# Layer 2's end columns on GpSimd, Scharr smoothing from two-row sums, x2 stored in a step of its own, and new step lists in a four-layer convolution kernel

## The chip, the cores and the metric

The kernel runs on one core of a Trainium2 chip. The metric is the time of one execution on the device in microseconds, median of several runs. Names used below: PE is TensorE, DVE is VectorE, ACT is ScalarE, POOL is GpSimd, SP is the engine that here only issues DMAs. POOL issues DMAs too.

## What is computed

The input x is 16 images of 64 channels with 128 x 128 points, float32. Four layers follow, each of the form x = x + f(gn(x)), with gn a group norm over pairs of channels.

```python
# layer 0: gram = xf xf^T / N ; f = conv_w (gram xf)
# layer 1: f = |Kx * v| + |Ky * v|,  Kx = [[3,0,-3],[10,0,-10],[3,0,-3]], Ky = Kx^T up to sign
# layer 2: temporal shift (a quarter of the channels one column left, a quarter one right), 3x3 conv, + b
# layer 3: y = 3x3 conv with w_bin, 1x1 conv, batch norm over all 16 images, leaky relu, clip(0, 255)
```

Layer 3's batch norm needs the sums over all images, so the last part of it can start only when every image has passed the 3x3 convolution.

## The kernel before, in words

**Tiles.** An image is cut into 8 tiles of R = 8 rows per half image; 128 partitions are 64 channels times two halves. Each image passes four stages, one tile or one pair of tiles per step of the main loop: Gram (products for layer 0), Front (layers 0 and 1, one tile a step; `x`, `po`, `xh`, `u`, `e` are its tiles), Layer2 and Layer3 (two tiles a step; `v`, `dA`, `dB`, `q`, `one`, `two`, `c`). Several images are under way at once. From step FIRST + LAG on, the work repeats every eight steps, that is once per image: four steps with pairs of Layer 2, called (False, 0) to (False, 3) in the code and F0 to F3 here, then (True, 3), (True, 0), (True, 1), (True, 2) with pairs of Layer 3, T3, T0, T1, T2 here. Front works on tile 0 of an image in T1, tile 1 in T2, tiles 2 to 5 in F0 to F3, tile 6 in T3, tile 7 in T0. After the last step comes the tail: batch norm coefficients, the end of layer 3 read back from HBM, and for six images (`AGAIN`) layer 3's convolution a second time (`v_again`, `two_again`).

**Order of the work.** The dictionary ORDER (line 27) gives each kind of step a list of parts; `for name in ORDER[kind_of(step)]` (line 1282) calls the parts in that order, and every engine and every DMA queue runs its instructions in the order in which they were called (class InOrder, line 124; all operations go through its line 134, so the profile shows L134 for nearly all of them). "a" and "b" are the first and second tile of a pair: "load a" and "load b" fetch tiles for the pair after next, "near a", "near b" and "far a" norm them, "d a" and "d b" form the differences, "a one", "a own" and "section" are the matmuls, "a sum" adds the partial results, "a sq" squares for the statistics, "a out" stores. "stencil", "smooth", "slope", "abs", "x +", "+ y" are the six parts of Scharr. "0" to "3" are four phases in which Gram and the chains of small products advance.

**Scharr** (line 736). "stencil" makes u = 3 v[1:R+2] + v[0:R+1] on R + 1 rows, 128 x 1170 elements, and e = v[2:R+2] - v[0:R], 128 x 1040. "smooth" makes u = 3 u + u[next row], which is 3, 10, 3 over three rows, and a first step of the column smoothing of e. "slope" takes differences, "abs" is on ACT, "x +" and "+ y" add x and the two absolute values; the result, x2, lies in the tile u, of which there are two buffers.

**x2's store** (part "x2" in Front.at, line 682, and Front.store, line 766). In the step after the one that made it, x2 is stored with two DMAs issued by SP, and in the same part ACT squares it. A buffer of u may be written again only when its store and its square are done.

**Gram's loads** (line 571). In the second step of an image's Gram the first three loads (`xr`, 512 KB each) are issued by SP together in phase 0; each further one follows the use of an earlier one.

**Layer2.norm** (line 957). ACT norms a loaded tile of (R + 1) rows. The temporal shift needs two corrections: the two end columns, times a channel mask, go into a tile `edges`, 9 rows for either side (two ACT instructions), and in the tile itself the first and last column are multiplied by masks (two more). **Layer2.combine** (line 1022) adds `edges` to the end columns of `two` in PSUM, in two DVE instructions because the lower 64 partitions take rows 1 to 8 and the upper ones rows 0 to 7, and then forms x3. `different` (line 929) takes the difference of neighbouring rows of the normed tile on DVE and, for the second of a pair, copies part of it with two DMAs issued by POOL (`q`). `one` (line 984) is the first matmul on the normed tile.

**The tail's first norm** (line 1334). In phase 2 of the last step the first tile of the second pass is normed by ACT (`again_in`, line 1225).

Of the kernel before, what the change touches and what calls it, by code (L numbers as in the profile page):

```python
# [10 lines left out]
F32 = mybir.dt.float32  # L11
AF = mybir.ActivationFunctionType
# [12 lines left out]
PARTS = SCHARR + ("x", "mix", "mix b", "rows a", "rows b", "x2")  # L25
# [3 lines left out]
        "a one", "0", "x", "rows b", "load a", "stencil", "mix", "a c", "b sum", "a own", "b sq", "wi",  # L29
        "near b", "smooth", "slope", "1", "x2", "section", "close", "d b", "a sum", "b one", "abs", "rows a",  # L30
        "x +", "2", "b out", "a out", "b own", "a sq", "b c", "mix b", "mean", "scale", "far a", "d a",
        "load b", "+ y", "3",
    ],
    (False, 1): [
        "x", "rows b", "a one", "load a", "b sum", "0", "stencil", "b sq", "wi", "mix", "a c", "near b", "x2",
        "smooth", "a own", "close", "slope", "section", "b out", "abs", "rows a", "1", "d b", "a sum", "mean",
        "2", "x +", "b one", "a out", "mix b", "b c", "scale", "a sq", "b own", "far a", "d a", "load b", "+ y",
        "3",
    ],
    (False, 2): [  # L40
        "x", "rows b", "a one", "load a", "stencil", "b sum", "smooth", "0", "a c", "mix", "a own", "b sq",
        "wi", "near b", "x2", "close", "b out", "section", "slope", "1", "b one", "d b", "mean", "abs",
        "rows a", "a sum", "far a", "x +", "2", "mix b", "b c", "scale", "a sq", "a out", "d a", "load b",
        "+ y", "b own", "3",
    ],
    (False, 3): [
        "x", "rows b", "a one", "load a", "stencil", "b sum", "0", "mix", "a c", "a own", "b sq", "wi",
        "smooth", "near b", "slope", "section", "b out", "close", "x2", "d b", "mean", "a sum", "abs", "rows a",
        "a out", "1", "x +", "2", "load b", "b one", "d a", "+ y", "b own", "mix b", "b c", "a sq", "scale",
        "3",  # L50
    ],
    (True, 3): [
        "rows b", "stencil", "x2", "a one", "load a", "0", "b sum", "b sq", "mix", "a own", "smooth", "a c",
        "close", "mean", "scale", "slope", "b out", "x", "section", "1", "abs", "near a", "near b", "rows a",
        "b one", "b c", "a sum", "x +", "2", "b own", "load b", "wi", "a sq", "a out", "mix b", "+ y", "d a",
        "d b", "3",
    ],
    (True, 0): [
        "rows b", "x2", "a one", "a own", "b sum", "0", "stencil", "b sq", "load a", "smooth", "close", "a c",
        "near a", "mean", "slope", "x", "1", "mix", "section", "abs", "near b", "rows a", "wi", "b out", "2",  # L60
        "b one", "b c", "a sum", "scale", "x +", "b own", "far a", "d a", "d b", "a sq", "a out", "+ y",
        "load b", "mix b", "3",
    ],
    (True, 1): [
        "a one", "x2", "rows b", "load a", "b sum", "a own", "0", "stencil", "near b", "b sq", "close",
        "smooth", "d b", "a c", "slope", "1", "b out", "x", "mix", "section", "mean", "scale", "abs", "rows a",
        "2", "a sum", "x +", "wi", "b one", "b c", "b own", "d a", "a sq", "a out", "+ y", "load b", "mix b",
        "3",
    ],
    (True, 2): [  # L70
        "rows b", "a one", "b sum", "0", "stencil", "b sq", "load a", "x2", "1", "smooth", "a own", "close",
        "mean", "slope", "b out", "x", "a c", "near a", "mix", "abs", "section", "near b", "b one", "b c",
        "rows a", "a sum", "wi", "2", "x +", "a sq", "load b", "scale", "a out", "b own", "far a", "d a", "d b",
        "+ y", "mix b", "3",
    ],
    "fill": [
        "x", "a one", "b sum", "rows b", "load a", "stencil", "0", "a own", "b sq", "x2", "mix", "smooth",
        "slope", "b out", "close", "near b", "section", "d b", "a c", "mean", "1", "rows a", "wi", "abs",
        "a sum", "x +", "mix b", "b one", "2", "+ y", "b c", "a out", "load b", "b own", "d a", "a sq", "scale",
        "3",  # L80
# [90 lines left out]
def tile_kernel(ctx: ExitStack, tc: tile.TileContext, x, cw_h, w2_t, b2, wbin_t, w1_t, b1, gamma, beta, consts, out):  # L171
# [10 lines left out]
    def k(name):  # L182
        return kc[:, AT[name][0]:AT[name][1]]
# [75 lines left out]
    def chunk_tile(name):  # L259
        return ring.tile([P, (R + 2) * W], F32, tag="v", name=name, bufs=4)  # L260
# [296 lines left out]
    class Gram:  # L557
# [5 lines left out]
        def at(self, i, q):  # L563
            b = self.b
            n = 4 * (i - NS) + q

            self.part({1: 44, 5: 42, 9: 42}.get(n, 0))
            if n == 10:
                chains.append(gram_chain(b, self.pg))

            if i == 1 and q == 0:
                for m in range(3):
                    self.load(m)
            m = {11: 0, 13: 1, 15: 2, 17: 3, 19: 4, 21: 5, 23: 6, 25: 7}.get(4 * i + q)
            if m is not None:
                rows_to_columns(b, m, self.xr.pop(m))
                if m + 3 < NS:
                    self.load(m + 3)
# [45 lines left out]
    class Front:  # L624
        first, last = -3, NS

        def __init__(self, b):
            self.b, self.xs, self.po, self.x2 = b, {}, {}, {}

            self.four = b >= EARLY  # L630
            self.st = stp.tile([P, 2, NS], F32, tag="st2", name=f"st2_{b}")
# [50 lines left out]
        def at(self, i, part):  # L682
# [41 lines left out]
            if part == "x2":  # L724
                if 1 <= i:
                    self.store(i - 1)
                    act.activation(
                        junk.rearrange("p (j w) -> p j w", w=W), self.x2.pop(i - 1), AF.Square,
                        accum_out=self.st[:, 1, i - 1:i],
                    )  # L730
                if i == NS:
                    quick.append(coefficients(self.st, lambda co: coefs2.update({b: co}), b2_sb))
# [3 lines left out]
        def scharr(self, i, n):  # L736
            v = self.chunk(i)
            if n == 0:
                self.u = work.tile([P, R + 1, W + 2], F32, tag="u", name=f"u_{self.b}_{i}")
                self.e = work.tile([P, R, W + 2], F32, tag="e", name=f"e_{self.b}_{i}", bufs=1)  # L740
                dve.scalar_tensor_tensor(
                    self.u, v[:, 1:R + 2, :], 3.0, v[:, 0:R + 1, :], op0=ALU.mult, op1=ALU.add
                )
                dve.tensor_sub(self.e, v[:, 2:R + 2, :], v[:, 0:R, :])
            h, p = self.u[:, 0:R, :], self.e[:, :, 0:W + 1]
            gx, gy = h[:, :, 0:W], p[:, :, 0:W]
            if n == 1:
                dve.scalar_tensor_tensor(h, h, 3.0, self.u[:, 1:R + 1, :], op0=ALU.mult, op1=ALU.add)
                dve.scalar_tensor_tensor(p, self.e[:, :, 1:W + 2], 3.0, p, op0=ALU.mult, op1=ALU.add)
# [3 lines left out]
            if n == 3:  # L753
                act.activation(gx, gx, AF.Abs)
                act.activation(gy, gy, AF.Abs)
# [4 lines left out]
            if n == 5:  # L760
                dve.scalar_tensor_tensor(
                    gx, gy, self.co[:, 3:4], gx, op0=ALU.add, op1=ALU.add, accum_out=self.st[:, 0, i:i + 1]
                )
                self.x2[i] = gx

        def store(self, i):
            d = planes(x2_d[self.b])
            for s in range(2):
                sp.dma_start(
                    d[:, s, i * R // 2:(i + 1) * R // 2, :],  # L770
                    self.x2[i].rearrange("p (j s) w -> p s j w", s=2)[:, s],
                )
# [116 lines left out]
    class Layer2:  # L889
# [67 lines left out]
        def norm(self, i):  # L957
# [7 lines left out]
            e = stp.tile([P, 2, R + 1], F32, tag="edges", name=f"edges_{self.b}_{i}", bufs=6)  # L965
            for side, at in ((0, 0), (1, W + 1)):
                n = at + R * W if at + R * W < (R + 1) * W + 2 else at + (R - 1) * W
                m = (n - at) // W + 1
                act.activation(e[:, side, 0:m], f[:, at:n + 1:W], AF.Copy, scale=self.co[:, 3 + side:4 + side])
            self.edges[i] = e  # L970

            act.activation(t[:, :, 0], t[:, :, 0], AF.Copy, scale=k("keep0"))
            act.activation(t[:, :, W - 1], t[:, :, W - 1], AF.Copy, scale=k("keep1"))
# [48 lines left out]
        def combine(self, i):  # L1022
# [3 lines left out]
            for rows, j in ((lo, 1), (hi, 0)):  # L1026
                dve.tensor_add(
                    ends[rows], ends[rows], e[rows, :, j:j + R].rearrange("p t (m n) -> p n m t", n=2)
                )
# [211 lines left out]
    for step in range(FIRST - 2, steps):  # L1241
# [40 lines left out]
        for name in ORDER[kind_of(step)]:  # L1282
# [30 lines left out]
            if step == start_of(B - 1) and q == 0:  # L1313
# [4 lines left out]
                rest(work, "u", [R + 1, W + 2], 2)  # L1318
# [15 lines left out]
            if step == last_one and q == 2:  # L1334
                v_again.extend(chunk_tile(f"v_again_{n}") for n in range(2))
                again_in(*todo[0][1:], loaded[0][0])

# [4 lines left out]
    while chains:  # L1342
        tick()
    rest(ring, "y", [2, CP, W], 2)
# [26 lines left out]
    act.activation(sd, var, AF.Sqrt)  # L1371
    r0 = pair("r0_bn")
# [122 lines left out]
```

## Time and profile before

| | |
|---|---|
| median of three runs | 2561.53 us (2560.76 to 2568.36) |
| the profiled execution by its own clock | 2563.73 us |
| its span, first to last instruction | 2562.0 us |
| mean granted TensorE clock | 0.976 |
| ACT busy / POOL busy | 2029.4 / 698.8 us |
| HBM read and written | 321.46 and 243.28 MB |

Three stretches follow each other: the fill until about 260 us, in which the first images enter; the repeating eight steps until about 1800 us, and then the last images until about 2176 us; the tail until 2562 us. A group in the profile is a line, an engine, an operation, and the tiles out<-in with their shape, then the count, the busy time, the mean of one in ns, and the idle time of the engine just before, with what ended it. In a list of waits the columns are the total in us, the number of waits and the longest. In a timeline they are start, duration, engine, line, operation. "SPq" and "POOL DMA_DIRECT2D" are DMA issues.

### The profile page before, as it was taken

To read this page: it belongs to the slowest core of one execution; us is meant where nothing else is said; L and a number is where in the kernel's file an instruction comes from. 1 tells how busy PE (TensorE), PEld (TensorE's weight loads), DVE (VectorE), ACT (ScalarE), POOL (GpSimd) and SP (SyncE) were. 2 spreads that over 40 slices of the span, in tenths; PEclk is the share of its full clock that TensorE was granted. 3 is DMA by queue.
4 is the path that set the end of the run, shared out by engine and by line. 5 is a ranking of instruction groups with operands and counts; after the bars stand their busy time and mean duration, and the time that the engine had idled before them with its cause. 6 is when DMAs were issued, how large, how long until landed. Compare 5 with 4: busy or idle time off the path is not lost. (4 is left out here: it accounts for less than half of the span.)

```text
span 2562.0 us, 52738 instructions
## 1 busy us (share of the span) xinstructions
PE 2425.1 (95%) x19286; PEld 938.8 (37%) x19286; DVE 2120.4 (83%) x2939; ACT 2029.4 (79%) x3253; POOL 698.8 (27%) x1254
## 2 busy tenths in 40 slices
PE   6587999999999999999999999999999999999996
PEld 5332333333333333434343434343333333333332
DVE  4999999999999999999999999999999634444333
ACT  4777888889797979797978888887888655787775
POOL 3241313131313132323232323232321310222222
PEclk8688999999999999999999999999999999999998
DMA  9776979796767676757576979776767688999998
GB/s 228 194 195 180 233 199 233 192 233 188 191 171 193 163 197 160 201 160 201 160 199 173 243 192 231 200 205 168 200 170 193 156 264 261 417 417 417 413 412 338
DMA packets 610577, 585.33 MB, mean 228 GB/s; under 512 B 48480, under 2 KB 521984, under 8 KB 610320
## 3 DMA queue, kind: packets, MB, share of 16 engines
q1 hardware_dynamic: 556752, 425.34, 58.0%
q0 software_dynamic: 53568, 156.63, 20.1%
q8 instruction: 153, 2.51, 0.4%
q14 instruction: 104, 0.85, 0.1%
HBM read 321.46 MB, written 243.28 MB: 220 GB/s over the span
## 5 line engine op out<-in xcount | busy, mean ns | idle before, releaser
L134 PE MATMUL two<-dA,w 64*64 64x512 f32 (+2 forms) x2304 | 533.9, 595 | 0.0
L134 PE MATMUL two_again<-v_again,w 64*64 64x508 f32 (+1 forms) x3456 | 376.6, 592 | 10.7 <-ACT v_again L134 10.7
L134 POOL DMA_DIRECT2D v<-x_d x480 | 238.8, 503 | 499.8 <-PE one L134 220.3
L134 PE MATMUL one<-v,w 128*64 128x508 f32 (+2 forms) x1600 | 360.8, 584 | 0.3 <-ACT c L134 0.3
L134 PE MATMUL one<-v,wi 128*64 128x508 f32 (+3 forms) x1536 | 346.8, 585 | 13.6 <-ACT c L134 13.5
L134 PE MATMUL two<-dB,w 64*64 64x512 f32 (+2 forms) x1536 | 353.5, 593 | 0.0
L134 DVE SCALAR_TENSOR_TENSOR e<-e 128x1032 f32<-128x1032 f32 (+1 forms) x256 | 313.4, 1224 | 0.0
L134 ACT ACTIVATE xh<-po,co 128x128 f32<-128x128 f32 (+1 forms) x480 | 274.1, 619 | 13.3 <-PE po L134 12.4
L134 PEld LDWEIGHTS two<-dA,w 64*64 64x64 f32 (+1 forms) x2304 | 148.9, 133 | 276.9 <-issue 269.3
L134 ACT ACTIVATE junk<-x 128x1024 bf16<-128x1024 f32 x128 | 134.9, 1054 | 117.0 <-DVE x L134 116.5
L134 PEld LDWEIGHTS two_again<-v_again,w 64*64 64x64 f32 x3456 | 131.7, 134 | 254.7 <-issue 227.9
L134 ACT ACTIVATE v<-v,co 128x1154 f32<-128x1154 f32 x128 | 171.8, 1343 | 60.7 <-DMA v<-x_d 58.9
L134 ACT ACTIVATE v<-x,co 128x1024 f32<-128x1024 f32 (+3 forms) x256 | 205.0, 846 | 3.8 <-POOL co L134 3.8
L134 PE MATMUL po<-x,abd 64*64 64x512 f32 (+1 forms) x1024 | 183.3, 621 | 23.7 <-ACT xh L134 18.4
L134 DVE SCALAR_TENSOR_TENSOR u<-xh 128x1170 f32<-128x1170 f32 x128 | 176.0, 1375 | 34.5 <-DMA x_d<-u 28.1
L134 DVE SCALAR_TENSOR_TENSOR y<-two,c 128x1024 f32<-128x1024 f32 x128 | 156.0, 1219 | 52.4 <-issue 20.6
L134 DVE TENSOR_TENSOR dB<-v 128x1024 f32<-128x1024 f32 (+1 forms) x128 | 152.1, 1188 | 39.8 <-ACT v L134 31.9
L134 PEld LDWEIGHTS one<-v,w 128*64 128x64 f32 x1600 | 107.5, 137 | 206.2 <-issue 170.1
L134 PEld LDWEIGHTS one<-v,wi 128*64 128x64 f32 x1536 | 102.8, 136 | 215.7 <-issue 159.4
L134 ACT ACTIVATE junk<-y 128x1024 bf16<-128x1024 f32 x128 | 135.1, 1055 | 55.0 <-DVE y L134 53.7
L134 PE MATMUL two<-q,cross 64*64 64x512 f32 (+1 forms) x768 | 169.6, 570 | 6.3 <-issue 5.7
L134 PE MATMUL two<-dA,wi 128*64 128x508 f32 (+1 forms) x768 | 175.0, 589 | 0.0
(228 smaller groups left out, 4253.5 us busy)
## 6 DMA issues: line engine op xcount, KB each, us to landing
x_d<-u SPq DMA_DIRECT2D x256, 256.0 KB, 4.9
x_d<-x SPq DMA_DIRECT2D x490, 128.0 KB, 3.7
xr<-in_x SPq DMA_DIRECT2D x120, 512.0 KB, 6.2
y_d<-y SPq DMA_DIRECT2D x320, 128.0 KB, 3.8
x<-in_x SPq DMA_DIRECT2D x128, 256.0 KB, 4.5
x<-in_x POOLq DMA_DIRECT2D x128, 256.0 KB, 4.9
end_x<-x_d SPq DMA_DIRECT2D x36, 512.0 KB, 17.5
xw<-x_d SPq DMA_DIRECT2D x33, 512.0 KB, 17.2
```

The costliest lines, as they stand in the source:

```text
L134: return self.tc.keep_in_program_order(call(*args, **kwargs))
```

## The change

Five things are done. (1) "stencil" writes u = v[2:R+2] + v[0:R] on R rows, "smooth" makes u = 10/3 v[1:R+1] + u, and "abs" multiplies the x part by 3. (2) In Layer2.norm the four ACT instructions on end columns become three POOL multiplications: two for `edges`, one for each half of the partitions and 8 rows, which puts the right rows in place already, and one for both masked columns. Layer2.combine adds `edges` in one DVE instruction. (3) "x2" is split: "x2 sq" squares, "x2 out" stores whatever results wait in a list `sent`; "+ y" appends to it. (4) Gram's first three loads are issued in phase 0 and phase 2 of its second step and in phase 0 of its third. All step lists are new. (5) The tail's first norm is called behind the square root of the batch norm's coefficients, and its two tiles are taken after the loop.

The diff, with three of the nine lists:

```diff
     (False, 0): [
-        "a one", "0", "x", "rows b", "load a", "stencil", "mix", "a c", "b sum", "a own", "b sq", "wi",
-        "near b", "smooth", "slope", "1", "x2", "section", "close", "d b", "a sum", "b one", "abs", "rows a",
-        "x +", "2", "b out", "a out", "b own", "a sq", "b c", "mix b", "mean", "scale", "far a", "d a",
-        "load b", "+ y", "3",
+        "b sum", "x2 sq", "a one", "0", "rows b", "a c", "mix", "near b", "stencil", "load a", "smooth", "b sq",
+        "a own", "close", "x", "1", "slope", "section", "2", "d b", "abs", "x +", "b one", "b out", "x2 out",
+        "a sum", "wi", "+ y", "rows a", "a out", "b own", "mix b", "mean", "b c", "scale", "d a", "a sq",
+        "far a", "load b", "3",
     ],
     (False, 1): [
-        "x", "rows b", "a one", "load a", "b sum", "0", "stencil", "b sq", "wi", "mix", "a c", "near b", "x2",
-        "smooth", "a own", "close", "slope", "section", "b out", "abs", "rows a", "1", "d b", "a sum", "mean",
-        "2", "x +", "b one", "a out", "mix b", "b c", "scale", "a sq", "b own", "far a", "d a", "load b", "+ y",
-        "3",
+        "x", "rows b", "a one", "mix", "0", "a own", "b sum", "stencil", "a c", "smooth", "b sq", "section",
+        "close", "near b", "slope", "load a", "x2 sq", "1", "mean", "d b", "wi", "2", "abs", "rows a", "a sum",
+        "b one", "b out", "x2 out", "x +", "b own", "mix b", "b c", "a out", "load b", "d a", "+ y", "scale",
+        "a sq", "far a", "3",
     ],
...
     (True, 3): [
-        "rows b", "stencil", "x2", "a one", "load a", "0", "b sum", "b sq", "mix", "a own", "smooth", "a c",
-        "close", "mean", "scale", "slope", "b out", "x", "section", "1", "abs", "near a", "near b", "rows a",
-        "b one", "b c", "a sum", "x +", "2", "b own", "load b", "wi", "a sq", "a out", "mix b", "+ y", "d a",
-        "d b", "3",
+        "stencil", "x2 sq", "a one", "rows b", "0", "mix", "b sum", "smooth", "a own", "b sq", "load a",
+        "close", "mean", "b out", "scale", "slope", "section", "a c", "1", "x", "abs", "b one", "near a",
+        "rows a", "wi", "near b", "b c", "a sum", "x +", "2", "a sq", "load b", "+ y", "a out", "b own",
+        "mix b", "d a", "d b", "x2 out", "3",
     ],
...
-            if i == 1 and q == 0:
-                for m in range(3):
-                    self.load(m)
+            m = {4: 0, 6: 1, 8: 2}.get(4 * i + q)
+            if m is not None:
+                self.load(m)
...
-            if part == "x2":
+            if part == "x2 out":
+                while self.sent:
+                    self.store(*self.sent.pop())
+            if part == "x2 sq":
                 if 1 <= i:
-                    self.store(i - 1)
                     act.activation(
...
-                self.u = work.tile([P, R + 1, W + 2], F32, tag="u", name=f"u_{self.b}_{i}")
+                self.u = work.tile([P, R, W + 2], F32, tag="u", name=f"u_{self.b}_{i}")
...
-                dve.scalar_tensor_tensor(
-                    self.u, v[:, 1:R + 2, :], 3.0, v[:, 0:R + 1, :], op0=ALU.mult, op1=ALU.add
-                )
+                dve.tensor_add(self.u, v[:, 2:R + 2, :], v[:, 0:R, :])
...
-                dve.scalar_tensor_tensor(h, h, 3.0, self.u[:, 1:R + 1, :], op0=ALU.mult, op1=ALU.add)
+                dve.scalar_tensor_tensor(h, v[:, 1:R + 1, :], 10.0 / 3.0, h, op0=ALU.mult, op1=ALU.add)
...
-                act.activation(gx, gx, AF.Abs)
+                act.activation(gx, gx, AF.Abs, scale=3.0)
...
                 self.x2[i] = gx
+                self.sent.append((i, gx))
...
-            e = stp.tile([P, 2, R + 1], F32, tag="edges", name=f"edges_{self.b}_{i}", bufs=6)
-            for side, at in ((0, 0), (1, W + 1)):
-                n = at + R * W if at + R * W < (R + 1) * W + 2 else at + (R - 1) * W
-                m = (n - at) // W + 1
-                act.activation(e[:, side, 0:m], f[:, at:n + 1:W], AF.Copy, scale=self.co[:, 3 + side:4 + side])
+            e = stp.tile([P, 2, R], F32, tag="edges", name=f"edges_{self.b}_{i}", bufs=6)
+            for rows, j in ((lo, 1), (hi, 0)):
+                g = f[rows, j * W:]
+                ends = bass.AP(tensor=g.tensor, offset=g.offset, ap=[list(g.ap)[0], [W + 1, 2], [W, R]])
+                pool.tensor_tensor(
+                    e[rows], ends, self.co[rows, 3:5].unsqueeze(2).to_broadcast([C, 2, R]), op=ALU.mult
+                )
             self.edges[i] = e
-            act.activation(t[:, :, 0], t[:, :, 0], AF.Copy, scale=k("keep0"))
-            act.activation(t[:, :, W - 1], t[:, :, W - 1], AF.Copy, scale=k("keep1"))
+            sides = t[:, :, 0:W:W - 1]
+            at = AT["keep0"][0]
+            pool.tensor_tensor(
+                sides, sides, kc[:, at:at + 2].unsqueeze(1).to_broadcast([P, R + 1, 2]), op=ALU.mult
+            )
...
-            for rows, j in ((lo, 1), (hi, 0)):
-                dve.tensor_add(
-                    ends[rows], ends[rows], e[rows, :, j:j + R].rearrange("p t (m n) -> p n m t", n=2)
-                )
+            dve.tensor_add(ends, ends, e.rearrange("p t (m n) -> p n m t", n=2))
...
-            if step == last_one and q == 2:
-                v_again.extend(chunk_tile(f"v_again_{n}") for n in range(2))
-                again_in(*todo[0][1:], loaded[0][0])
...
     while chains:
         tick()
+    v_again.extend(chunk_tile(f"v_again_{n}") for n in range(2))
...
     act.activation(sd, var, AF.Sqrt)
+    again_in(*todo[0][1:], loaded[0][0])
```

In the other six lists the same parts are reordered. "x2 out" stands behind "+ y" in the four T lists and ahead of it in the four F lists; in F2 "near b" comes before "slope" and "d b" after "x +", in F3 "near b" comes before "smooth" and "d b" after "slope".

## The prediction

> **What bounds the kernel now.** I read the busy lines and slices of the page first, then the busy time of one image, then the waits of VectorE, then the groups by shape.
>
> ```profile
> PE 2425.1 (95%) x19286; PEld 938.8 (37%) x19286; DVE 2120.4 (83%) x2939; ACT 2029.4 (79%) x3253; POOL 698.8 (27%) x1254
> ...
> PE   6587999999999999999999999999999999999996
> ...
> DVE  4999999999999999999999999999999634444333
> ```
>
> PE looks full all along, but its ends are modelled. DVE is at 9 from slice 2 to slice 31 and falls to a third only in the tail. So two engines compete for the role of the bound until about 2000 us; the last 380 us are another stage (417 GB/s in the slices). The stall of one stencil recurs at 951.43 and 1077.76 us: 126.3 us, one image of eight steps. Busy time in one such stretch:
>
> ```profile
> core 0: us, PE busy (x) PEld busy (x) DVE busy (x) ACT busy (x) POOL busy (x), PEclk, DMA share, GB/s
> 865.00:991.30 126.30, 124.16 (x988) 48.60 (x984) 121.58 (x172) 107.50 (x180) 37.05 (x67) 1.00 0.68 181
> ```
>
> DVE works 121.6 of 126.3 us, ACT 107.5, POOL 37. For PE I count matmuls of this stretch by shape and price them by their spacing: 360 of 128*64 with 508 or 512 columns run in twos (12 of them advance the chain by 2.56 us, 0.427 a pair): 76.9. 248 of 64x512 in fours at 0.43: 26.6. 36 of 381 to 384 columns: 4.8. Gram products 8.6, short ones 5.4 (their rows' busy time). Together about 122 us. So **DVE is the bound, PE is as close as 122**, and no gain beyond 4.3 us an image is to be had. What DVE waits for between 260 and 2000 us:
>
> ```profile
> DVE u L134 <- DMA x_d<-u: 24.5, 10, 3.2
> DVE dB L134 <- ACT v L134: 11.1, 12, 1.7
> ```
>
> One thing stands out: the stencil that waits until an x2 store has landed, 2.0 us an image on average. The issue queue shows why:
>
> ```profile
> 935.84 5.02 SPq L134 DMA_DIRECT2D xr<-in_x  x3
> 940.96 5.03 SPq L134 DMA_DIRECT2D x_d<-u  x2
> ```
>
> Three loads for Gram stand ahead of the two stores of tile 2 and hold SP for 5 us; the stores take another 5, and tile 4, whose buffer this is, waits 3.0 us.
>
> **The change part by part.** Both programs issue the same matmuls and the same DMAs; the new lists move them, and I price a move where a wait follows from it. F0 to F3 are the steps of Layer 2's pairs, T0 to T3 those of Layer 3's; an image passes T1, T2, F0 to F3, T3, T0 with its Scharr tiles 0 to 7.
>
> ```profile
> L134 DVE SCALAR_TENSOR_TENSOR u<-xh 128x1170 f32<-128x1170 f32 x128 | 176.0, 1375 | 34.5 <-DMA x_d<-u 28.1 <-ACT xh L134 4.9 <-ACT edges L134 1.6
> L134 DVE TENSOR_TENSOR e<-xh 128x1040 f32<-128x1040 f32 x128 | 158.3, 1236 | 0.0
> ...
> L134 DVE TENSOR_TENSOR two<-two,edges 64x16 f32<-64x16 f32 x256 | 47.1, 184 | 18.1 <-PE two L134 9.9
> ```
>
> *Smoothing.* The first op shrinks from 1170 to 1040 elements and becomes a plain add of two rows; its price is the row of e, which reads the same rows: 1375 - 1236 = 0.139 us. The second keeps 1040 elements and two inputs: 0. The factor 3 rides in the Abs on ACT: the same instruction. 8 x 0.139 = 1.1 us an image.
>
> *Ends.* Two adds on 64 partitions become one on 128 with the same 16 elements: 0.184 saved per tile, 8 x 0.184 = 1.5 us. Both sit on the bounding engine: **-2.6 us an image**.
>
> *x2 stores and Gram loads.* The loads are spread over three phases, so the burst goes: -2.0. But a stall comes back elsewhere. "x2 out" empties a list from its end. In step T3 it stands behind "+ y", so tiles 5 and 6 go out together, 6 first, and the built program gives tile 7 the buffer of tile 6. From the end of tile 6's "+ y": second store issued after 0.5, landing 4.9 by the table of issues: 5.4 us. DVE has beside it dA and dB (2.3), the small vv and dd (1.0), one y (1.2): 4.5. New wait 0.9 (0 to 3). In the other steps the stores stand half a step or more ahead of the reuse. Net **-1.1**. SP's other issues change places with neighbours only (tile 2's stores now follow x3's).
>
> *Ends of Layer 2 on POOL.* ACT loses four instructions of 0.30 per tile, 131 us in all. DVE waits on ACT 13 us in 1740, so I book 0 (bound: 13 gained). What counts is the latency from norm to the zeroed sides: on ACT 4 instructions in 1.03 us. On POOL three, one after the other. The trace shows POOL with such small ops:
>
> ```profile
> 612.40 1.22 DVE L134 SCALAR_TENSOR_TENSOR y<-two,c 128x1024 f32<-128x1024 f32 x1
> ...
> 613.01 0.27 POOL L134 TENSOR_SCALAR co<-me,co 128x1 f32<-128x1 f32 x1
> ...
> 613.54 1.29 DVE L134 SCALAR_TENSOR_TENSOR u<-xh,co,u 128x1024 f32<-128x1024 f32 x1
> ...
> 613.65 1.33 POOL L134 TENSOR_SCALAR edge_upper<-co,kc 128x2 f32<-128x2 f32 x1
> ```
>
> Beside y, whose first input is PSUM, a POOL op takes 0.27 (others 0.18). Beside u, with two SBUF tensors, it ends 0.15 after u ends: it is held for the whole op. u itself is not longer (1.29; its group's mean is 1.28). So a tile costs POOL between 3 x 0.18 = 0.5 and 3 x 1.33 = 4.0 us. I take 3.1 (half an op, then two whole ones), because the Scharr ops, all with SBUF inputs alone, fill most of DVE's time. POOL goes from 37 to 62 us an image: far from full. The extra latency of 2.1 us is covered in most steps: between "near b" and "d b" F0 has six Scharr ops, F3 four, F2 three (3.6 us). It shows in F1: there POOL's half of the load of the second tile now stands behind the edges of the first ("far a", then "load b"). Chain from the end of F0's "a sum": a sq 1.2, norm 1.3, edges 0.5 to 3.1, issues and landing 5.0, norm 1.3, edges 0.5 to 3.1: 9.8 to 15.0. DVE reaches its dB after "+ y" 1.3, dA 1.1, the ends 0.2, the sum x 1.2 and six Scharr ops 6.9: 10.7 us. That is 0 to 4.3 late; while DVE waits it no longer holds POOL, so I take **+1.0** an image. Also behind waiting edges stand q copies and x loads, wanted a step later.
>
> Cost to DVE of POOL's reading: 0 by the row above; at most 0.14 per POOL op by the one u<-xh of 1.51 us beside copies of 192 elements, 3.3 an image. Mine have 16 or 18 elements: I take 0.
>
> The Trainium skill, GPSIMD Engine Reference, section 8 (Key points), warns against this very move: GpSimd shares its SBUF interfaces with VectorE and contends with instructions of two SBUF inputs. It does not say who pays; by the rows above POOL does. In its section 3.1 the same page gives 2.6 cycles an element at 1.2 GHz; an estimate from it, 18 elements in 0.04 us on top of the fixed part, would make a tile 0.7 us, quicker than ACT, and the sum 12 us lower.
>
> *Tail.* The first norm (0.28 + 0.49 + 1.24 on ACT at 2152) moves behind the root. ACT was waiting there, and the last square waited for y, not for it: nothing gained. ACT's first product comes 0.9 later: +1 (0 to 3).
>
> **Sum.** -2.6 - 1.1 + 1.0 = -2.7 an image: 123.6, above PE's 122. From 260 to 1800 us there are 12.2 images: -33. In the fill and the last images (30 tiles, 0.139 + 0.184 each = 9.7, DVE 92 and 98% busy): half, -5. Tail +1. Together -37: the profiled execution, 2563.7 us by its own clock, span 2562.0, becomes 2526.7. It lies 2.2 above the median 2561.5, so I forecast **2525**.
>
> **Rivals.**
>
> *PE's limit is reached.* No new stall at tile 7 nor in F1; each image falls to 122: -4.3 x 12.2 - 5 = -57, 2505. For it: DVE idles only 4.7 us an image. Against: three stalls must all be hidden.
>
> *Given back.* DVE's savings turn into waits for PE and POOL, F1 at its full 4.3 late: -2.6 - 1.1 + 4.3 = +0.6 an image, +7 - 5 + 1: 2564, no change. For it: PE has only 4 us to give.
>
> *POOL late, slower.* One queue holds edges, loads and q copies in order. If the three held ops are not covered, each such tile costs 4.0 - 1.0 = 3.0 us on DVE's difference and PE's first product. It decides from 3.7 / 3.0 = 1.3 uncovered tiles of the eight in an image. With two: +6.0 - 3.7 = +2.3 x 12.2 = +28, less 4: 2586. For it: POOL already idles 190 us on loads that wait for PE's "one", with the edges now behind some of them. Against: "near b" stands earlier in F0 and F3 than before.
>
> **How the numbers follow.** Forecast 50% (own range 2508 to 2543), PE's limit 20%, given back 12%, POOL late 18%. The range goes down to PE's limit with an error of 1.2 us an image in my count, 2490, and up towards two uncovered tiles, 2578; DVE's bound for POOL's reading (+40) lies inside it. About 0.3% is what a measurement of this kernel can tell from no change; so faster 0.70, same 0.12, slower 0.18.
>
> **What would show it.** DVE's add u at 1.24 and one add of ends at 0.18, each 128 times; 117 to 120 us of DVE in an image of 123 to 124; no wait of a stencil on x_d at tile 4, a wait of about 1 us at tile 7; POOL's edges near 1.2 us beside two-SBUF ops and 0.2 otherwise; dB waiting for POOL once an image. Wrong if an image stays near 126, if dB or PE's "one" wait on POOL in several steps, or if u lengthens beside POOL.

## The result, and the profile after

The changed kernel takes **2592.2 us** (median of 4 runs, 2587.7 to 2598.3), the kernel before 2562.6 in the same session: 1.0113 times as long, 95% interval 1.0084 to 1.0142. The forecast was 2525, 67 us lower; the range ended at 2578. The sign was wrong. The profiled execution has a span of 2585.9 us, 23.9 more than before.

First the page of the changed kernel: busy time of each engine, then the slices of PE and DVE.

```profile
PE 2443.8 (95%) x19286; PEld 950.9 (37%) x19286; DVE 2079.6 (80%) x2811; ACT 1905.4 (74%) x2741; POOL 913.5 (35%) x1638
...
PE   6578999999999999999999999999999999999996
...
DVE  5989999999998999899989999999999634443333
```

DVE works 40.8 us less, as meant, and the kernel is longer all the same: four of DVE's slices now show 8 where they showed 9. So the change gave DVE waits, not work. One image in the same steps (stretches of time: length, then busy time of PE, PEld, DVE, ACT, POOL, then clock, DMA share, GB/s):

```profile
821.70:950.40 128.70, 125.80 (x986) 50.05 (x984) 119.02 (x164) 99.34 (x147) 50.01 (x90) 1.00 0.71 178
```

Over the ten images from step to step between 438 and 1720 us an image takes 128.2 us on average, against 126.4 before. DVE is busy 119.1 of it, against 121.6. The ten images hold 18 of the 23.9 us; the stretch before them is 1.7 longer, the last images 1.0, the tail, counted here from DVE's first y of the last image (at 2004 us in the kernel before), 3.1. What DVE waits for between 260 and 2000 us of the changed kernel (total us, times, longest):

```profile
DVE u L134 <- DMA x_d<-u: 53.5, 29, 4.0
DVE dB L134 <- POOL v L134: 18.0, 23, 2.7
DVE co L134 <- PE bank L134: 7.8, 10, 1.3
DVE two L134 <- PE two L134: 7.4, 8, 3.0
DVE dB L134 <- DMA v<-x_d: 5.3, 12, 0.4
```

The wait of a stencil on an x2 store, forecast to go from 24.5 to about 11, went to 53.5. I counted the idle time in front of each stencil from the trace, tile by tile (the n-th add of u belongs to tile n mod 8). Per image, and with DVE's wait in front of dB as well:

| us an image | before | forecast | after |
|---|---|---|---|
| DVE busy | 121.6 | 119.0 | 119.1 |
| stencil of tile 4 waits for the store of tile 2 | 2.4 | 0 | 2.9 |
| stencil of tile 7 waits for a store | 0 | 0.9 | 1.55 |
| stencil of tile 6 waits | 0 | 0 | 0.6 |
| dB around tile 3 waits for POOL | 0 | 1.0 | 1.0 |
| dB around tile 4 waits for ACT | 1.1 | 1.1 | 0 |
| dB around tiles 1 and 2 | 0 | 0 | 0.8 |
| co of tile 3 waits for PE's bank | 0 | 0 | 0.65 |

Here co are small coefficients that DVE copies out of a PSUM bank when PE has filled it. Of tile 7's 1.55, 0.27 end with ACT (`junk`, the squares) and not with the store. The rows account for the miss in one image, 128.2 against a forecast of 123.6: 4.15 more for stores, 0.8 and 0.65 new, 0.1 of DVE's work, 1.1 less for ACT, together 4.6.

Here is the store of tile 2 on SP in the changed kernel, at the place that the prediction showed of before:

```profile
936.02 2.61 SPq L134 DMA_DIRECT2D x_d<-x  x4
...
940.93 1.50 SPq L134 DMA_DIRECT2D xr<-in_x  x1
...
944.56 5.56 SPq L134 DMA_DIRECT2D x_d<-x  x4
950.16 1.28 SPq L134 DMA_DIRECT2D x_d<-u  x2
```

And DVE, the last op of tile 2's x2 and the stencil of tile 4:

```profile
935.90 1.28 DVE L134 SCALAR_TENSOR_TENSOR u<-e,co,u 128x1024 f32<-128x1024 f32 x1
...
957.01 1.24 DVE L134 TENSOR_TENSOR u<-xh 128x1040 f32<-128x1040 f32 x1 [1.72 <-DMA x_d<-u]
```

The burst of three loads is gone (one xr here). But x2 is ready at 937.1, and its store is issued at 950.2: in the list of F1 "x2 out" is the 28th item, behind "b out", whose four x_d<-x stores hold SP for 5.6 us, 2.1 of them waiting for a DVE op. The old list had "x2" as its 13th.

**The held POOL ops** came out as read. In the changed kernel, POOL's first edges op runs into a two-input DVE op with SBUF inputs, and so does its op on the sides:

```profile
912.92 1.59 POOL L134 TENSOR_TENSOR edges<-v,co 64x16 f32<-64x16 f32 x2 [1.24 <-issue]
913.19 1.25 DVE L134 TENSOR_TENSOR u<-u 128x1024 f32<-128x1024 f32 x1
914.36 1.24 DVE L134 SCALAR_TENSOR_TENSOR e<-e 128x1024 f32<-128x1024 f32 x1
...
914.60 1.08 POOL L134 TENSOR_TENSOR v<-v,kc 128x18 f32<-128x18 f32 x1
```

The sides' op starts 0.24 us into DVE's op on e (914.36 to 915.60) and ends at 915.68, 0.08 after it. Of all 384 such ops of the trace 217 take 0.21 to 0.25 us, nearly all while DVE is idle or at x or y from PSUM (12 start up to 0.2 us ahead of a DVE op with two SBUF inputs, and are not held); 165 take up to 1.31 us and end 0.06 to 0.10 us after a DVE op with two SBUF inputs; two in the fill fit neither. From the end of the norm to the end of the sides a tile takes 2.3 us on average (0.9 to 5.7, 96 tiles), against 1.09 on ACT in the kernel before.

### The profile page after: what moved, and what is told of

It reads as the page before. It is cut to its first block, busy times and chain, and to the rows that moved or that the text cites. A ratio compares the mean times of both kernels' runs of the same rounds, so it can differ in the third digit from the quotient of the medians.

```text
span 2585.9 us, 52765 instructions
## 1 busy us (share of the span) xinstructions
PE 2443.8 (95%) x19286; PEld 950.9 (37%) x19286; DVE 2079.6 (80%) x2811; ACT 1905.4 (74%) x2741; POOL 913.5 (35%) x1638
## 4 chain that ended last, share of the span: by engine, by line
PE 53%; DVE 17%; DMA 15%; issue 5%; ACT 5%; POOL 3%; SPq 2%; DVEq 0%; POOLq 0%; ACTq 0%
PE two L134 22%; PE one L134 15%; PE two_again L134 9%; DVE u L134 7%; DVE e L134 5%; DMA x_d<-u 4%; PE bank L134 3%; PE po L134 3%; DMA end_x<-x_d 3%; DMA v<-x_d 2%; SPq L134 2%; DMA q<-dB 1%; DVE y L134 1%; POOL v L134 1%; POOL edges L134 1%
## 5 line engine op out<-in xcount | busy, mean ns | idle before, releaser
L134 PE MATMUL two<-dA,w 64*64 64x512 f32 (+2 forms) x2304 | 542.2, 601 | 0.0
L134 PE MATMUL two_again<-v_again,w 64*64 64x508 f32 (+1 forms) x3456 | 375.8, 592 | 11.1 <-ACT v_again L134 11.1
L134 POOL TENSOR_TENSOR edges<-v,co 64x16 f32<-64x16 f32 x256 | 149.8, 585 | 248.3 <-ACT v L134 183.4
L134 POOL TENSOR_SCALAR va<-nv 128x1 f32<-128x1 f32 x64 | 51.6, 806 | 494.3 <-DVE nv L134 471.7
L134 ACT ACTIVATE u<-u 128x1024 f32<-128x1024 f32 x128 | 135.5, 1059 | 117.1 <-DVE u L134 117.1
L134 PE MATMUL two<-q,cross 64*64 64x512 f32 (+1 forms) x768 | 185.2, 587 | 32.1 <-DMA q<-dB 14.8
L134 DVE TENSOR_TENSOR u<-xh 128x1040 f32<-128x1040 f32 x128 | 158.4, 1238 | 69.1 <-DMA x_d<-u 56.9
L134 PE MATMUL po<-x,abd 64*64 64x512 f32 (+1 forms) x1024 | 194.7, 625 | 19.5 <-ACT xh L134 12.6
```

The source lines that it names most:

```text
L134: return self.tc.keep_in_program_order(call(*args, **kwargs))
```

## The experiments

All thirteen at a glance. "Image" is the mean of the same ten images; the ratio is to the kernel before, with its 95% interval. "Parts" are the smoothing, the spread Gram loads and the tail's later norm.

| kernel | lists | ends on | us | ratio | image |
|---|---|---|---|---|---|
| before | old | ACT | 2563 | 1 | 126.4 |
| after | new | POOL | 2592.2 | 1.0113 (1.0084 to 1.0142) | 128.2 |
| out_f1 | new, "x2 out" first in F1 | POOL | 2564.7 | 1.0015 (1.0002 to 1.0027) | 126.0 |
| out_first | new, "x2 out" first | POOL | 2549.8 | 0.9951 (0.9936 to 0.9966) | 124.6 |
| first_loadb | the same, "load b" earlier in F0 | POOL | 2537.4 | 0.9904 (0.9889 to 0.9919) | 124.2 |
| first_loadb_q | the same, q copies on SP | POOL | 2546.0 | 0.9933 (0.9912 to 0.9954) | 125.1 |
| first_act | as out_first | ACT | 2547.8 | 0.9947 (0.9931 to 0.9964) | 124.7 |
| ends_act | new | ACT | 2588.5 | 1.0101 (1.0086 to 1.0117) | 127.6 |
| old_lists | old, parts | POOL | 2619.3 | 1.0223 (1.0206 to 1.0240) | 129.3 |
| old_loadb | old, "load b" earlier, parts | POOL | 2572.3 | 1.0036 (1.0024 to 1.0047) | 126.0 |
| old_loadb_q | the same, q copies on SP | POOL | 2531.3 | 0.9879 (0.9865 to 0.9894) | 123.4 |
| parts_act | old, parts | ACT | 2523.2 | 0.9848 (0.9833 to 0.9862) | 123.1 |
| parts_one_add | the same, one add of ends | ACT | 2522.3 | 0.9845 (0.9831 to 0.9860) | 123.3 |
| gram_only | old, Gram loads alone | ACT | 2527.3 | 0.9863 (0.9848 to 0.9878) | 123.2 |
| scharr_only | old, smoothing alone | ACT | 2552.9 | 0.9961 (0.9948 to 0.9973) | 125.7 |

**out_f1: one item of one list.** Theory: the late x2 store is the loss. Rival: PE's products are next anyway.

```diff
     (False, 1): [
-        "x", "rows b", ...
+        "x2 out", "x", "rows b", ...
-        "b one", "b out", "x2 out", "x +", ...
+        "b one", "b out", "x +", ...
```

> The changed kernel, but the item "x2 out" of the list of step F1 alone stands first instead of behind "b out". Store theory: the stencil of tile 4 waits 2.9 us an image (31.9 us in 11 images) because tile 2's x2 store is issued only at 950.2, behind eight x_d<-x issues; its x2 is finished at 937.1 and SP idles before that. Issued 10 us earlier, it has landed: wait 0, image 128.2 - 2.9 = 125.3, time 2592 - 32 = 2560. Rival, PE's order: PE shows 125.8 busy of 128.2, so DVE would run into PE's products instead (co from the bank, the adds of ends); the image stays at 127 or more and the time above 2580. Rival, POOL: dB at tile 3 waits for POOL as before (1.0 us) and takes no more; this run does not touch it.

Measured: 2564.7, 27.6 us less than the changed kernel; the stencil of tile 4 waits no more. The store theory forecast 32 less, the rival at most 12. The image lost 2.2 us, not 2.9: 0.7 came back, for the x2 op of tile 4's steps now waits for ACT's abs (7.6 us in all), and the dB at tile 3 waits longer. The store of tile 2, whose x2 is ready at 925.4 here, now goes out 3.2 us later and not 13:

```profile
928.64 0.93 SPq L134 DMA_DIRECT2D x_d<-u  x2
```

**out_first: the same in all eight lists.**

> The changed kernel, but "x2 out" stands first in all eight lists (not in the fill's), so that each tile's x2 is stored at the start of the next step, one at a time. Store theory: tile 4's wait (2.9 us an image) and tile 7's (1.55) both go: 128.2 - 4.45 = 123.7, time 2592 - 32 - 19 = 2541. Rival, PE's order: at most what separates 128.2 from PE's 125.8 busy can be won, so not below 2592 - 29 = 2563, with new waits of DVE on PE. No theory has it slower than the changed kernel, unless the x2 stores now hold SP in front of the loads of v: then ACT's norms wait longer than 41 us in all and dB waits on ACT.

Measured: 2549.8, another 14.9 less, and 0.5% faster than before. The waits of DVE in this kernel, 260 to 1800 us:

```profile
DVE dB L134 <- POOL v L134: 23.5, 25, 4.5
DVE u L134 <- ACT u L134: 15.6, 23, 2.9
DVE co L134 <- PE bank L134: 6.7, 8, 1.3
```

No stencil waits for x_d any more: the 53.5 us of the changed kernel are gone. 42 of the 67 us by which the forecast missed are the place of "x2 out". The 2563 that PE's rival put as the floor is passed.

**old_lists: the new code in the old lists.**

```diff
-    (the eight lists and the fill's of the change)
+    (those of before, each "x2" split into "x2 out", "x2 sq")
```

> The code of the change (ends on POOL, sum of two rows, spread Gram loads, later first norm of the tail) with the lists of before; where they say "x2", "x2 out" and "x2 sq" follow each other. Store theory (the lists lose, the parts gain): tile 4's store has its old place and no burst of loads ahead of it, so the stalls of tiles 4 and 7 are at most 0.5 us; DVE 119.0 busy, dB waits 1 to 3 us for POOL: an image of 121 to 123.5 and 2490 to 2525 us. POOL theory (the late ends lose): with the old lists the POOL ops stand where nothing was arranged for them; dB and PE's "one" wait for POOL in several steps, the image is 126 or more and the time 2560 or more.

Measured: 2619.3, and the POOL theory holds here: dB at tile 4 waits 5.6 us an image. POOL's queue in this kernel, around one such wait, and then DVE:

```profile
970.09 1.10 POOL L134 TENSOR_TENSOR edges<-v,co 64x16 f32<-64x16 f32 x2 [1.32 <-ACT v L134]
971.27 0.22 POOL L134 TENSOR_TENSOR v<-v,kc 128x18 f32<-128x18 f32 x1
971.48 3.02 POOL L134 DMA_DIRECT2D v<-x_d  x6
...
981.63 0.52 POOL L134 TENSOR_TENSOR edges<-v,co 64x16 f32<-64x16 f32 x2 [6.28 <-ACT v L134]
982.23 0.22 POOL L134 TENSOR_TENSOR v<-v,kc 128x18 f32<-128x18 f32 x1
```

```profile
982.48 0.96 DVE L134 TENSOR_TENSOR dB<-v 128x768 f32<-128x768 f32 x1 [5.66 <-POOL v L134]
```

POOL is free at 968.8, but its next item is the ends of tile a, and they wait for ACT's norm. Only then does it issue the six DMAs of "load b". ACT's norm of b starts at 980.2, when the last of them have landed (up to 5.8 us after issue), the ends of b follow, and dB, which DVE wanted at 976.8, starts at 982.5. The ops on the ends are short (1.1 and 0.5 for both edges, 0.22 for the sides): it is the **wait in front of them** that the loads inherit.

**ends_act: the new lists with the old ends.** Edges and sides as in the kernel before, four ACT copies a tile, two adds on DVE.

```diff
-                pool.tensor_tensor(e[rows], ends, ...)
+                act.activation(e[:, side, 0:m], f[:, at:n + 1:W], AF.Copy, ...)
...
-            dve.tensor_add(ends, ends, ...)
+            for rows, j in ((lo, 1), (hi, 0)):
+                dve.tensor_add(ends[rows], ends[rows], ...)
```

> The changed kernel with the ends of Layer 2 back on ACT (four copies of 0.3 us a tile) and the two adds of 64 partitions. POOL theory: dB's waits at tiles 1, 2 and 3 (0.4, 0.4, 1.0 us an image) and the wait of co for PE's bank at tile 3 (0.65) come from the late ends and go: -2.5, the two adds cost DVE 8 x 0.18 = +1.5: 127.2, about 2580. Store theory: the stalls of tiles 4 and 7 stay (4.4 us an image), DVE has 1.5 us more, and only dB's 1.0 goes: +0.5 an image, 2592 to 2600; ACT at 109 us an image stays far from full.

Measured: 2588.5, between the two theories and, within the intervals, the same as the changed kernel. dB's waits at tile 3 fell from 12.4 to 3.3 us, and the stencil's at tile 4 from 31.9 to 19.0, which neither theory had. What they gave was taken by co behind them (7.8 to 11.1 for PE's bank) and by DVE's second add.

**parts_act: the old lists with the old ends.** Beside ends_act only the lists differ, beside old_lists only the ends.

> Before with the sum of two rows (smoothing), the Gram loads spread over three phases and the tail's later norm: lists of before, ends on ACT with two adds, each x2 stored where it was. Burst theory of the prediction: tile 4's stall (2.4 us an image in before) goes with the three loads ahead of the store, DVE falls by 1.1: 126.4 - 3.1 to 3.5 = 123, time 2563 - 40 = 2523. Rival: the store stays late because x_d<-x issues and not the loads hold SP: stall 2, image 125.3, time 2550. Rival, PE: 122 to 124 an image is its floor, about 2535.

Measured: 2523.2. That is what I had forecast for the whole change, but by luck: here the ends stay on ACT and the lists are the old ones. So with ACT's ends the new lists cost 65 us (2523 to 2588), and with the old lists POOL's ends cost 96 (2523 to 2619); the new lists are 27 better than the old ones where POOL has the ends.

**old_loadb: one item ahead of another.**

```diff
-        ... "scale", "far a", "d a", "load b", "+ y", "3",
+        ... "scale", "load b", "far a", "d a", "+ y", "3",
```

(in F0; likewise in F1 and F2, where "load b" also passes "a out")

> The kernel old_lists (code of the change, lists of before; 2619 us, dB at tile 4 waits 5.6 us an image for POOL) with "load b" put directly ahead of "far a" in F0, F1 and F2. Queue theory: what costs there is not the length of the held ops but that POOL's six DMAs of "load b" stand behind the ends of tile a, so behind ACT's norm: issued at 971.5 to 974.5, they land at 980.2. Ahead of the ends, they go out 2.6 us earlier or more; of the 5.6 us at most 2 stay, image 129.3 - 3.6 to 5.6 = 123.7 to 125.7, time 2550 to 2575. Rival, the held ops: POOL takes 2.3 us from the norm to the sides where ACT took 1.0, so 1.3 us of the 5.6 are due to that and stay; then the time is above 2600.

Measured: 2572.3, 47 less; dB at tile 4 waits 1.25 us an image in place of 5.6. So the order in POOL's queue was 4.3 of it. (The waits are those of the profiled execution, at 2563.7 the fastest of the ten.) That the 1.25 left are the longer way from norm to sides on POOL is not shown: with the ends on ACT the same dB, over the same twelve images, waits 1.0 us an image in the kernel before and 0.9 in parts_act. Behind it PE shows the second victim of the same queue:

```profile
PE two L134 <- DMA q<-dB: 17.6, 11, 4.3
```

**old_loadb_q: the q copies off that queue.**

```diff
-                    pool.dma_start(flat(q2[cols(1 - k), n]), ...)
+                    sp.dma_start(flat(q2[cols(1 - k), n]), ...)
```

> The kernel old_loadb (2572 us) with the q copies (128 DMAs of dB) issued by SP instead of POOL. Queue theory: the adds of ends at tile 2 wait 2.5 us an image for PE's two, which waits for q: the copy stands in POOL's queue behind the ends of tile b (1 to 3.5 us late). From SP it goes out when dB is done: 126.0 - 1.5 to 2.5, time 2542 to 2555. Rival: SP, which waits in order for x and u, holds the copies as long or longer, or delays the x2 stores behind them: 2570 or more, with DVE waiting on x_d<-u again.

Measured: 2531.3, 41 less, more than the 17 to 30 expected, and 1.2% faster than before with the ends still on POOL. PE waits 1.4 us for q in place of 17.6, and the adds of ends 0.6 for PE in place of 29.6.

**first_loadb and first_loadb_q: the same two steps in the new lists.** First "load b" goes ahead of "far a" in F0, then q to SP.

> The kernel out_first (2550 us) with "load b" ahead of "far a" in F0. Queue theory: dB at tile 3 waits 1.3 us an image behind norm a, ends a, load b, norm b, ends b; the load issued ahead of norm a lands some 2 us earlier: wait 0 to 0.7, image 124.6 - 1 = 123.6, time 2537. Rival, PE's order: co waits 0.55 us for PE's bank right behind this dB, and PE is busy 123.9 of 124.6; the wait moves there and the time stays at 2545 to 2550.

Measured: 2537.4, the time that the queue theory has (12.4 less; dB at tile 3 from 15.9 to 7.2 us), but in part by luck. Of the 14.6 us between the two profiled executions the ten images give 3.6 (124.6 to 124.2 an image, forecast 123.6), and 9.2 lie before them; and co's waits for PE's bank grew from 6.7 to 8.6 us, as the rival says.

> The kernel first_loadb (2537 us: the changed kernel with "x2 out" first and "load b" ahead of "far a" in F0) with the q copies issued by SP. It still lies 14 us above parts_act (2523), at 124.2 us an image against 123.1. Queue theory: the rest of the loss is again POOL's order (PE's two waits 0.5 us an image for q, adds of ends and co wait for PE): 123.2 to 123.6 an image, 2524 to 2530. Rival: the rest comes from other moves of the lists (co's products, abs on ACT behind junk): 2533 to 2540, with u waiting for ACT and co for the bank as before.

Measured: 2546.0; my theory fell. PE waits for q no more, yet DVE's waits are worse:

```profile
DVE u L134 <- ACT u L134: 41.7, 26, 4.5
DVE dB L134 <- POOL v L134: 22.6, 28, 2.7
```

ACT itself waits 111.6 us for loads of v, against 53.6 in first_loadb, and its abs of u, which DVE wants, stands behind that norm. The trace shows SP, which holds the copies, issuing its loads later: in nine images its first load of v for that norm goes out 3.2 to 5.1 us after tile 4's stencil starts, against -0.3 to 3.6 in first_loadb. SP waits in all 145.0 us for a dB (3.6 in first_loadb):

```profile
SPq L134 <- DVE dB L134: 145.0, 49, 5.4
```

No run takes this apart from the rest of SP's order. The last 14 us between the mended new lists (2537) and parts_act stay unassigned.

**first_act: the ends once more, in the mended lists.** out_first with the ends of ends_act.

> The kernel out_first with the ends of Layer 2 back on ACT and the two adds of 64 partitions. Held-op theory: dB's waits at tiles 1 to 3 (0.6, 0.4, 1.3 us an image) shrink by about 1.5 in all, DVE has 1.5 more (8 x 0.18): same within 5 us, 2545 to 2555. If the POOL ends were the real loss of the change it falls by 2 us an image or more, below 2527; if they were a gain it rises above 2562.

Measured: 2547.8 against 2549.8: the same. In these lists, with the x2 stores early, the ends on POOL cost and save nothing against ACT. POOL's queue is not yet in order in either ("load b" stands behind "far a" in F0); the move of first_loadb was not tried with the ends on ACT.

**gram_only, scharr_only, parts_one_add: the single gains.** The first is before with

```diff
-            if i == 1 and q == 0:
-                for m in range(3):
-                    self.load(m)
+            m = {4: 0, 6: 1, 8: 2}.get(4 * i + q)
+            if m is not None:
+                self.load(m)
```

the second is before with the two smoothing ops and the Abs of the change, the third is parts_act with one DVE add, for which ACT writes the shifted halves with four copies.

> Before with the three Gram loads of xr spread over three phases (4, 6, 8) and nothing else. Burst theory: tile 4's stencil waits 2.4 us an image in before because three loads stand ahead of the x2 store of tile 2; spread, the store goes out some 4 us earlier, the stall goes: 126.4 - 2.0 to 2.4 an image, 2535 to 2540. Rival: the whole gain of parts_act (40 us) is DVE's shorter smoothing and the store stays late: 2555 to 2563.

> Before with the smoothing from sums of two rows (and the factor 3 in ACT's Abs), and nothing else. Additive theory: DVE 1.1 us an image less, of which the ops between tile 2's x2 and the stencil of tile 4 are eaten by the stall: 0.9 to 1.1 an image, 2550. Rival, the stall swallows it: the store of tile 2 is set by SP's queue and not by DVE, so the stall at tile 4 grows by what DVE saves and the time stays at 2560 to 2565.

> The kernel parts_act (2523 us) with one add of the ends on 128 partitions in place of two on 64; ACT writes the two shifted halves itself, with four copies of edges a tile in place of two. DVE falls by 8 x 0.18 = 1.5 us an image, to 119.1 of 123.1; ACT rises by 16 x 0.3 = 4.8 to 112. If DVE is still the bound: 122, time 2508. If PE's floor of 122 to 123 is reached (it shows 122.9 busy of 123.1): 2520 to 2525. If the 0.6 us more from norm to sides shows at dB of tile 4 (which waits 1.0 us for ACT): 2525 to 2535.

Measured: 2527.3, 2552.9 and 2522.3. Spreading three loads gives 36 us by itself, more than expected: the stall of 2.4 us an image at tile 4 goes, dB's waits fall from 12.3 to 6.9 us, the stretch before the ten images is 3.5 shorter. In gram_only one load stands ahead of tile 2's store, which goes out 3.7 us after its x2 is done, against 8.3 in the kernel before, and holds SP for 1.2 us in place of 5.0:

```profile
918.30 0.42 SPq L134 DMA_DIRECT2D xr<-in_x  x1
918.83 1.21 SPq L134 DMA_DIRECT2D x_d<-u  x2
```

The smoothing alone gives 10 us; the stall at tile 4 stays at 27.3 us in it. Both together give 39.5, not 46, and the one add gives nothing more. This is the stretch of one image in parts_one_add:

```profile
563.00:686.30 123.30, 122.97 (x988) 48.59 (x986) 118.81 (x164) 110.97 (x196) 36.11 (x66) 1.00 0.75 194
```

PE is busy 122.97 of 123.30, DVE 118.8. Four kernels end at the same image, 123.1 to 123.4 us, with DVE busy for 121.5 (gram_only), 120.6 (parts_act), 118.9 (old_loadb_q) and 118.9 of it (parts_one_add): so it is not DVE's work that sets it. That PE's matmuls do is argued, from the count of 122 and from PE's busy time, 122.8 to 123.2 in all four; no run takes matmuls away.

## Why the prediction was wrong

**The step that failed is the x2 stores.** I wrote: "In the other steps the stores stand half a step or more ahead of the reuse. Net -1.1." I had checked the one place with two stores in a row, T3, and there I was right in kind and low in size (tile 7 waits 1.55, forecast 0.9). For F1 I read the item's place in the list and not its time on SP. The store is issued 13 us after its x2 is done and 5.1 before DVE is free for the stencil; issue and landing take 6.8. So the -2.0 did not come and +0.5 did. With the 0.6 at tile 6, another late store that I had not seen, the term is +2.65 an image (0.5 + 1.55 + 0.6) in place of -1.1, 46 us over 12.2 images. out_f1 and out_first together give back 42.4.

**The burst.** That the three loads delay the store was right, and underestimated: 36 us alone, where -2.0 an image makes 24. It was lost again in the changed kernel because four other issues took their place in front of the same store.

**Smoothing and ends.** Right as busy time: u at 1.238 and one add at 0.176, 128 times each; DVE down 2.5 an image, forecast 2.6. As time they were worth less than the full price that I gave them: the smoothing 10 us alone, the one add nothing. From the list of groups of the changed kernel, by shape:

```profile
L134 DVE TENSOR_TENSOR u<-xh 128x1040 f32<-128x1040 f32 x128 | 158.4, 1238 | 69.1 <-DMA x_d<-u 56.9 <-ACT xh L134 7.3 <-ACT junk L134 4.1
L134 DVE TENSOR_TENSOR two<-two,edges 128x16 f32<-128x16 f32 x128 | 22.5, 176 | 23.3 <-PE two L134 23.2
```

**POOL's latency.** The wait at dB of tile 3 came out at the +1.0 that I took, by the chain that I wrote down; a tile takes 2.3 us on POOL, a little under my 3.1. What I missed are the dB at tile 1 (0.4), whose wait goes with the ends back on ACT, and the q copies in the same queue, for which PE's two waits 14.8 us in all. (The 0.4 at tile 2 stays in ends_act and first_act, so it comes with the new lists and not from POOL.) I named "q copies and x loads, wanted a step later" and gave them no price; in the old lists their price was 41 us. The rival "POOL late" came near the number (2586), but by luck: the same lists with the ends on ACT take 2588.5. Its mechanism is what happens in the old lists; in the new ones the move in POOL's queue is worth 12.4 us (first_loadb) and the stores' place 42.4.

**DVE's price for POOL's reading.** The 0 was nearly right: u<-u takes 1.221 us alone and 1.231 with one of POOL's ops beside it.

The Trainium skill, GPSIMD Engine Reference, section 8 (Key points), warns of contention at the SBUF interfaces that GpSimd shares with VectorE, when a VectorE instruction has two SBUF inputs; the runs agree and say who pays here: POOL almost all of it. The estimate of 0.7 us a tile from its section 3.1 is near the quickest tile (0.9: three ops of 0.21 to 0.25 us and the gaps between them) and far below the mean (2.3), for the hold has no part in it.

**ACT's relief.** I booked 0. first_act and out_first are the same, which fits, but that pair changes ACT's relief, POOL's latency and DVE's second add at once.

**PE's limit.** The count of 122 was good: 123. So the most that could be had was 40 us, and the forecast of 37 off was nearly all of it: it could hold only if no new wait at all appeared.

**Tail and fill.** From the start of DVE's last y to the end the kernel before takes 407.9 us, gram_only and scharr_only, also without the later norm, 407.1 and 407.4, and the twelve kernels with it 406.5 to 408.4: a cost of +1 is not to be seen. The 3.1 us by which the changed kernel's tail is longer lie ahead of that y; what causes them stays open. The stretch before the ten images gained the 5 us in parts_act (431.3 for 436.5) and lost them in the changed kernel (438.2).

## What to carry to other kernels

An item's place in a hand-written list says nothing about when its DMA goes out: follow the issuing queue, item by item, up to the moment the reused buffer is wanted, for every store that the change moves and not only for the one that looks suspicious. A small op given to an engine that also issues DMAs costs its queue the wait in front of it, and every DMA behind it inherits that wait; look for those DMAs first and move them ahead. When several parts are changed at once, run the parts alone: here three spread loads held almost all of the gain, and the new lists hid it, most of all by the place of the x2 stores.

## What the runs showed of the hardware

The hold of POOL was more exact than I had read it from a few rows: no op of 16 or 18 elements a partition that overlapped such a DVE op to its end got away sooner than 0.06 us after it, while DVE's own op (u<-u) grew by 0.01 us. And a single list item, or three loads issued in three phases instead of one, moves this kernel by 28 and 36 us. All the DVE work that the change takes away is 40.8 us of busy time, of which scharr_only's share gave 10 and the one add nothing.
